# A graph layer stack on one core: the short group of edges moved to the front, adjacency steps moved, row norms of the convolutions on GpSimd, waits of pools by tile

## The chip, the cores and the metric

The kernel runs on one core of one Trainium2 chip. The metric is the device time of one execution in microseconds, as the median of several runs. The engines are called by their short names in the profile: PE (TensorE; PEld are its weight loads), DVE (VectorE), ACT (ScalarE), POOL (GpSimd) and SP (SyncE, here only a DMA queue).

## The reference

There are 1250 nodes of 512 features and 41250 edges (20000 drawn ones in both directions and a loop on each node), sorted by receiver. Two layers follow each other; all is float32.

```python
edge_index = jnp.stack([src, dst])
xn = _layernorm(x, axis=-1)
x = x + gnn0(xn, edge_attr_4, edge_attr_8, edge_index, ...) + mix0(xn, ...)   # messages over edges; linear attention
x = x + ffn0(_layernorm(x), ...)                                              # 8 experts, the best 2 of each node
xn = _layernorm(x, axis=-1)
x = x + gnn1(xn, edge_index, W1, b1, W2, b2) + mix1(xn, ...)                  # two graph convolutions; linear attention
x = x + ffn1(_layernorm(x), ...)                                              # 6 experts, one weighting for all nodes

# gnn0: a product of sender features with edge attributes and a small network's weights, summed by receiver
msg0 = jax.ops.segment_sum(m0, receiver, num_segments=num_nodes)
# gnn1, each of its two convolutions:
norm = dinv[src] * dinv[dst]            # dinv = 1/sqrt(degree), degree from dst
out = jax.ops.segment_sum((x @ W)[src] * norm[:, None], dst, num_segments=n) + b   # then relu
```

## The kernel before

Nodes lie in 10 tiles of 125 rows (`R`, `NT`); `X` holds all of them in SBUF. Edges lie in 323 tiles of 128 (`ET`), and tiles in 47 groups of 7 (`GW`, `NG`). 323 is 46 x 7 + 1: the last group has one tile. The program is written with a framework that draws the semaphores itself and orders each engine's instructions: what is written later may be put earlier on its engine where its inputs allow it. `tc.issue_after(mm.ins)` ties the TensorE instructions of a block behind a matmul, and no other engine's.

The stages, in order of time:

1. **Norm and senders** (to about 53 us). `piece(a, b)` norms the node tiles in four pieces (`PIECES`) and `sender` writes the gather table `xup`. Meanwhile `dg` takes in the receivers, one group to a partition (spare places filled with N by a memset), and the least and greatest receiver of each group give `base`, the group's window of 32 receivers. `rel` is each edge's receiver less that base.
2. **Edges** (about 65 to 591 us), `edges`. Two tiles at a time: `product` gathers sender rows on POOL's queue (`sg`, L443) and multiplies the network's output with `w4b` into `pw` (L448); `messages` makes `msg` on DVE (L454, L457); `gather` multiplies `msg` with the group's factors `sy` into the bank `pd` (L591 to L597). `factors(g)` makes `sy` for a group: two DVE operations and two small ACT multiplies for each tile (L436), in three buffers. At a group's last tile `pd` is copied to `sm` (L601) and added to the table `agg` in HBM by an indirect DMA (L602). Scatters into one table wait for each other, since windows overlap.
3. **Node outputs and router** (591 to about 716 us). `outputs(t)` starts `pz` from a map (L664), reads `agg` back on SP's queue (`ag`, L93/L94 through the helper `spread`), transposes it (L677) and adds. A conditional further pass over the edges stands ahead of it (L640); these data don't take it. `route` and the code after it choose the experts.
4. **Experts** (716 to 1449 us). `unit(u)` takes 256 rows through one expert: 16 steps of first-layer matmuls and a gelu each (L971, L972), then 16 steps of second-layer matmuls (L979). Units 0 to 4 have `counts(g)` among their steps: for each tile of a group a one-hot of receivers times a one-hot of senders (L201), copied to `sa` (L203) and added to the table `adj` in HBM (L204), so `adj` becomes the matrix of edge counts. In unit 5 (`u == NA`) `adjacency(d)` reads node tile d of it back (`ad`, on POOL's queue, two buffers), adds the loop (L932), sums the degrees (L933), casts one half each on DVE and ACT to bf16 (`adb`, one buffer, L936/L937) and transposes it (L943) into `At`. Result rows go to `xrow` by an indirect add (L991). `weights` loads the experts on SP's queue.
5. **Convolutions** (1461 to about 1750 us). Degrees give `dc` (1/sqrt in its second column) and the row `dr`. Node tile by node tile X is read back, normed and scaled into `xs`, and `parts` splits `xs` into three bf16 parts on ACT, POOL (`r`, L1127) and DVE. The plain norm `xn` is transposed into `xT` for the attention. The first aggregation (L1175) takes the node tiles as they come: 12 matmuls for each against the first 500 columns of `At`. The maps L1086 and L1093 and the second aggregation (L1191) follow.
6. **Attention and last experts** (1750 us to the end).

Pools are stacked: a pool that is opened takes the memory of pools closed before it, and its tiles wait for everything in those pools.

Of the kernel before, what the change touches and what calls it, by code (L numbers as in the profile page):

```python
# [20 lines left out]
N = 1250  # L21
# [10 lines left out]
HID = 64  # L32
GW = 7
NG = -(-ET // GW)
W = 32
NPAD = N + W
LO = 313
# [19 lines left out]
def tile_graph_layers(ctx: ExitStack, tc: tile.TileContext, i: dict, out: bass.AP):  # L57
# [1 line left out]
    V, S, T, G = nc.vector, nc.scalar, nc.tensor, nc.gpsimd  # L59

    def pool(stack, name, bufs=1, space=None):
        return stack.enter_context(tc.tile_pool(name=name, bufs=bufs, **({"space": space} if space else {})))

    dram = pool(ctx, "dram", space=DRAM)
    cst = pool(ctx, "cst")
# [18 lines left out]
    def tr_tile(name):  # L84
        return ps_tile("tr", name)
# [5 lines left out]
    def spread(engine, dst, src, at=112):  # L91

        engine.dma_start(dst[:at], src[:at])  # L93
        engine.dma_start(dst[at:], src[at:])  # L94
# [85 lines left out]
    def by_tile(table):  # L180

        return table.rearrange("(c n) f -> n c f", c=4)[:N, :, :].rearrange("(p t) c f -> p t c f", t=NT)

    def counts(sp, g, code, idx, bank):

        n, t0 = min(GW, ET - g * GW), g * GW
        sh = sp.tile([P, GW, P], F16, tag="sh", name="sh")
        q = [P, n, P]
        V.tensor_tensor(sh[:, :n], io[:, None, :].to_broadcast(q), code[:, t0:t0 + n, None].to_broadcast(q),
                        op=OP.is_equal)  # L190
        pa = ps_tile(bank, "pa")
        for j in range(n):
            lo = sp.tile([P, LO + 1], F16, tag="los", bufs=4, name="los")
            if j < 2:

                ab = sp.tile([P, LO + 1], F16, tag="ab", name="ab")
                S.activation(ab, iol, AF.Abs, bias=slo[:, 1, t0 + j:t0 + j + 1], scale=1.0)
                S.activation(lo, ab, AF.Relu, bias=1.0, scale=-1.0)
            else:
                V.tensor_scalar(lo, iol, slo[:, 0, t0 + j:t0 + j + 1], None, op0=OP.is_equal)  # L200
            T.matmul(pa[:, :LO], sh[:, j, :], lo[:, :LO], start=j == 0, stop=j == n - 1)  # L201
        sa = sp.tile([P, LO], F32, tag="sa", bufs=3, name="sa")
        S.copy(sa, pa[:, :LO])  # L203
        G.indirect_dma_start(  # L204
            out=adj[:, :], out_offset=bass.IndirectOffsetOnAxis(ap=idx[:, g:g + 1], axis=0),
            in_=sa, in_offset=None, compute_op=OP.add)

    with ExitStack() as s0:
# [8 lines left out]
        G.dma_start(wu[:, 0, :], i["L0_gnn_W_up0"])  # L217
        G.dma_start(wu[:, 1, :], i["L0_gnn_W_up1"])
        dg = ec.tile([NG, GW * P], I32, name="dg")
        G.memset(dg, N)  # L220
        full = ET // GW
        dr_ = i["dst_row"]
        spread(G, dg[:full, :], dr_[:full * GW * P].rearrange("(g e) -> g e", e=GW * P), full // 16 * 16)
        if full < NG:
            G.dma_start(dg[full:, :(ET - full * GW) * P], dr_[None, full * GW * P:])
        dstc = ec.tile([P, ET], I32, name="dstc")
        G.dma_start(dstc, i["dst_cols"])
        srcc = ec.tile([P, ET], I32, name="srcc")
# [101 lines left out]
        with tc.issue_after(last[0].ins):  # L330
# [33 lines left out]
            EP = NG * GW  # L364
            rel = ec.tile([P, EP], F32, name="rel")
            V.memset(rel, 0.0)
            V.tensor_copy(rel[:, :ET], dstc)
# [13 lines left out]
            def window(code, idx):  # L381

                V.tensor_scalar(bs, base[:, 0, :], float(N), rows, op0=OP.min, op1=OP.add)
                V.tensor_copy(idx, bs)
                V.tensor_scalar(cd[:, 0, :], rel[:, :ET], 0.0, None, op0=OP.is_ge)
                V.scalar_tensor_tensor(cd[:, 0, :], rel[:, :ET], float(W), cd[:, 0, :], op0=OP.is_lt, op1=OP.mult)
                V.scalar_tensor_tensor(cd[:, 1, :], shi, float(W), rel[:, :ET], op0=OP.mult, op1=OP.add)
# [35 lines left out]

        def factors(g):

            n, t0 = min(GW, ET - g * GW), g * GW
            oh = ew.tile([P, GW, W], F32, tag="oh", bufs=3, name="oh")
            V.tensor_tensor(oh[:, :n, :], io[:, None, :W].to_broadcast([P, n, W]),  # L428
                            rel[:, t0:t0 + n, None].to_broadcast([P, n, W]), op=OP.is_equal)
# [148 lines left out]
        def edges(first, idx):  # L578
# [3 lines left out]
            def gather(t, msg):  # L582


                g, j = t // GW, t % GW
                if j == 0:
                    now["d"] = mm_tile("pd")
                sy, d = mask[g], now["d"]
                q = dict(start=j == 0, stop=j == GW - 1 or t == ET - 1)
                mf = msg.rearrange("p b a u -> p (b a) u")  # L590
                T.matmul(d[:W, :SW], sy[:, j, 0, :], mf.rearrange("p a u -> p (a u)")[:, :SW], **q)  # L591
                for c in range(1, 4):
                    T.matmul(d[c * W:(c + 1) * W, :2 * P], sy[:, j, c, :], mf[:, 4:5 + c:c, :],  # L593
                             start=j == 0, stop=False, skip_group_check=True)
                for c in range(1, 4):
                    a = SW + (c - 1) * 64
                    T.matmul(d[c * W:(c + 1) * W, 2 * P:SW], sy[:, j, 0, :], mf.rearrange("p a u -> p (a u)")[:, a:a + 64],  # L597
                             start=False, stop=q["stop"], skip_group_check=True)
                if q["stop"]:
                    sm = ew.tile([P, SW], F32, tag="sm", bufs=5, name="sm")  # L600
                    S.copy(sm, d[:, :SW])  # L601
                    G.indirect_dma_start(  # L602
                        out=agg[:, :], out_offset=bass.IndirectOffsetOnAxis(ap=idx[:, g:g + 1], axis=0),
                        in_=sm, in_offset=None, compute_op=OP.add)
# [7 lines left out]
            for t in range(0, ET, 2):  # L612
# [6 lines left out]
                    ef[b + 2] = attrs(b + 2)  # L619
                if first and at == 10 and b and b - 1 < len(steps):  # L620
                    steps[b - 1]()
                g = t // GW + 1
                if g < NG and g not in mask:
                    mask[g] = factors(g)
                got = [product(x, h[b]) for x in two]
                for x in ready:
                    gather(*x)
# [94 lines left out]
    with ExitStack() as s3:  # L722
# [223 lines left out]
        def unit(u, hu, xu):  # L946
# [6 lines left out]
                    work.setdefault((2 * n + 1) * 16 // len(gs_), []).append(lambda g=g: counts(fk, g, code0, idx0, "acc"))  # L953
            if u == NA:
                for d in range(NT):
                    work.setdefault(8 + (7 * d) // 3, []).append(lambda d=d: adjacency(d))
            n = [0]

            def step(mm):
# [98 lines left out]
    with ExitStack() as s1:  # L1058
# [38 lines left out]
        with ExitStack() as s3:  # L1097
# [24 lines left out]
            def parts(dst, t, src):  # L1122

                d = [x[:R, t, :] for x in dst]
                r = gw.tile([P, D], F32, tag="r", name="r")
                S.copy(d[0], src)
                G.tensor_tensor(r[:R], src, d[0], op=OP.subtract)  # L1127
                S.copy(d[1], r[:R])
                V.tensor_tensor(d[2], r[:R], d[1], op=OP.subtract)
# [7 lines left out]
            g2 = [load_g(i["L1_gnn_W2"][a * 512:(a + 1) * 512, :]) for a in range(2)]  # L1137
            nc.sync.dma_start(gb1, i["L1_gnn_b1"])
            row_bcast(gb2, i["L1_gnn_b2"])
            for t in range(NT):  # L1140
                st = gw.tile([P, V.BN_STATS_DIM], F32, tag="bst", bufs=3, name="n3s")
                V.bn_stats(st[:R], X[:R, t, :])
                V.bn_aggr(mv1[:R, t, :], st[:R])
                S.activation(rs1[:R, t:t + 1], mv1[:R, t, 1:2], AF.Sqrt, bias=eps[:R], scale=1.0)
                V.reciprocal(rs1[:R, t:t + 1], rs1[:R, t:t + 1])
                sc = gw.tile([P, 2], F32, tag="sc", bufs=3, name="sc")
                V.tensor_tensor(sc[:R, 0:1], rs1[:R, t:t + 1], dc[:R, t, 1:2], op=OP.mult)
                V.scalar_tensor_tensor(sc[:R, 1:2], mv1[:R, t, 0:1], -1.0, rs1[:R, t:t + 1], op0=OP.mult, op1=OP.mult)
                xs = gw.tile([P, D], F32, tag="xs", name="xs")
                V.tensor_scalar(xs[:R], X[:R, t, :], mv1[:R, t, 0:1], sc[:R, 0:1], op0=OP.subtract, op1=OP.mult)  # L1150
                parts(xs_, t, xs[:R])
                xn = gw.tile([P, D], F32, tag="xn", bufs=1, name="xn1")
                S.activation(xn[:R], X[:R, t, :], AF.Identity, bias=sc[:R, 1:2], scale=rs1[:R, t:t + 1])
                ps = tr_tile("ptr")
                v = ps[:, :4 * R].rearrange("p (k r) -> p k r", k=4)
                for k in range(4):
                    T.transpose(v[:, k, :], xn[:R, k * P:(k + 1) * P], ident[:R, :R])
                S.copy(xT[:, :, t * R:(t + 1) * R], v)

            def mapped(t, pp):  # L1160
                p_ = gw.tile([P, D], F32, tag="xs", name="prf")
# [435 lines left out]
```

## Time and profile before

| | |
|---|---|
| median of 3 runs | 2175.81 us (2175.56 to 2176.47) |
| the profiled execution's own time | 2173.73 us |
| its span, first to last instruction | 2171.9 us |
| mean granted TensorE clock | 0.973 |
| busy: PE, DVE, ACT, POOL | 2039.8, 891.1, 640.7, 635.3 us |
| 590.6 to 607.7 us: PE busy | 6.57 of 17.1 us |
| unit 5, 1149.3 to 1226.4 us: PE busy | 67.41 of 77.1 us |
| unit 6, 1226.4 to 1282.0 us: PE busy | 55.60 of 55.6 us |
| 1449.5 to 1469.2 us: PE busy | 4.90 of 19.7 us |

The profile is of one execution, and its times count from its first instruction. A row of its timeline gives the start, the duration, the engine, the line, the operation with output and inputs, how often it was done in a row, and in brackets how long the engine had been idle before it and what ended that. "L93" and "L94" are the two halves of `spread`, whoever calls it. In the slices a digit is a share in tenths, and PEclk is the clock that TensorE was granted.

### The profile page before, as it was taken

The numbers are of one execution on the slowest core, as the hardware profiler recorded it, in microseconds if no ns is written. First come the engines' busy times: TensorE is split into PE (matmuls) and PEld (weight loads), VectorE is DVE, ScalarE is ACT, GpSimd is POOL, SyncE is SP. The second block draws the span as 40 slices with busy tenths as digits, with TensorE's granted clock in tenths as the row PEclk, the third lists the DMA queues.
The fourth block names the chain that finished last, engine by engine and source line by source line (L and its number), as shares of the span: only waits on it lengthen the run. The fifth ranks groups of instructions, "written<-read, shape, count | busy, mean of one in ns | idle before, by whom it ended". The sixth has DMA issues, their size and how long they took to land. (4 is left out here: it accounts for less than half of the span.)

```text
span 2171.9 us, 29920 instructions
## 1 busy us (share of the span) xinstructions
PE 2039.8 (94%) x11341; PEld 1109.4 (51%) x11341; DVE 891.1 (41%) x1864; ACT 640.7 (29%) x1665; POOL 635.3 (29%) x589
## 2 busy tenths in 40 slices
PE   7899999989886899999998999978999999999999
PEld 5334444434364646565566666644446655444354
DVE  7688888868757323232233300004000124670000
ACT  3443444434222424243343311115112121241000
POOL 1677777787600323222322211102000020002000
PEclk9899999989997899999999999989999999999999
DMA  8977777757653875958376312413001040200000
GB/s 257 309 203 179 203 200 189 191 137 189 156 146 104 268 225 153 280 145 239 70 235 165 71 25 64 141 31 111 1 0 64 15 95 0 65 7 1 14 14 19
DMA packets 132866, 270.60 MB, mean 125 GB/s; under 512 B 22028, under 2 KB 45396, under 8 KB 132569
## 3 DMA queue, kind: packets, MB, share of 16 engines
q0 software_dynamic: 48048, 124.53, 24.3%
q1 hardware_dynamic: 82952, 140.78, 20.3%
q10 hardware_dynamic: 1694, 3.07, 0.5%
q8 instruction: 99, 1.62, 0.3%
q14 instruction: 73, 0.60, 0.1%
HBM read 248.73 MB, written 44.76 MB: 135 GB/s over the span
## 5 line engine op out<-in xcount | busy, mean ns | idle before, releaser
L443 POOL DMA_INDIRECT sg<-xup,srcc x323 | 311.7, 965 | 165.9 <-issue 63.0
L457 DVE TENSOR_TENSOR msg<-pw,sg 128x768 f32<-128x768 f32 x323 | 305.4, 946 | 0.0
L971 PE MATMUL phd<-hu,ew 128*128 128x256 f32 x1280 | 292.9, 385 | 10.3 <-ACT hd L972 8.0
L979 PE MATMUL pye<-ew,hd 128*128 128x512 f32 x640 | 287.3, 593 | 0.0
L971 PEld LDWEIGHTS phd<-hu,ew 128*128 128x128 f32 x1280 | 243.8, 193 | 50.1 <-ACT hd L972 14.6
L591 PE MATMUL pd<-msg,sy 128*32 128x320 f32 x646 | 215.9, 448 | 29.3 <-DVE msg L457 28.5
L593 PE MATMUL pd<-msg,sy 128*32 128x256 f32 x1938 | 197.8, 394 | 0.0
L448 PE MATMUL pw<-w4b,h 64*128 64x512 f32 x646 | 187.0, 655 | 0.0
L979 PEld LDWEIGHTS pye<-ew,hd 128*128 128x128 f32 x640 | 117.5, 190 | 124.3 <-issue 122.8
L454 DVE TENSOR_TENSOR msg<-pw,sg 128x256 f32<-128x256 f32 x323 | 134.5, 416 | 78.0 <-PE pw L448 38.8
L436 ACT ACTIVATE sy<-oh,y 128x32 f32<-128x32 f32 x646 | 145.9, 312 | 6.1 <-DVE oh L428 3.3
L204 POOL DMA_INDIRECT adj<-sa,idx x47 | 81.6, 1736 | 220.4 <-ACT sa L203 122.9
L200 DVE TENSOR_SCALAR los<-iol,slo 128x314 f16<-128x314 f16 x230 | 58.2, 304 | 199.4 <-PE pa L201 199.4
L591 PEld LDWEIGHTS pd<-msg,sy 128*32 128x32 f32 x646 | 54.4, 109 | 161.5 <-DVE msg L457 93.6
L972 ACT ACTIVATE hd<-phd,b 128x256 f32<-128x256 f32 x160 | 75.8, 474 | 174.5 <-PE phd L971 174.5
L1414 PE MATMUL pyf<-w,hd 128*125 128x512 f32 (+1 forms) x280 | 125.1, 599 | 0.0
L991 POOL DMA_INDIRECT xrow<-yo,slot x23 | 36.3, 1577 | 298.6 <-ACT yo L990 284.9
L1400 PE MATMUL ph<-uT,w 128*128 128x500 f32 (+3 forms) x336 | 120.8, 515 | 1.1 <-ACT hd L1402 1.0
L989 DVE TENSOR_TENSOR yo<-pye,b 128x512 f32<-128x512 f32 x20 | 13.8, 690 | 244.4 <-PE pye L979 231.3
L597 PEld LDWEIGHTS pd<-msg,sy 128*32 128x32 f32 x1938 | 80.7, 112 | 56.0 <-issue 4.0
L412 ACT ACTIVATE h<-ph 128x512 f32<-128x512 f32 (+1 forms) x124 | 68.2, 591 | 135.5 <-PE ph L408 93.7
L597 PE MATMUL pd<-msg,sy 128*32 128x64 f32 x1938 | 94.1, 221 | 0.0
(424 smaller groups left out, 2650.1 us busy)
## 6 DMA issues: line engine op xcount, KB each, us to landing
ew<-in_L_ffn_W SPq DMA_DIRECT2D x104, 1024.0 KB
agg<-zero SPq DMA_DIRECT2D x12, 512.0 KB
adj<-zero SPq DMA_DIRECT2D x12, 512.0 KB
ag<-agg SPq DMA_DIRECT2D x10, 560.0 KB
ad<-adj POOLq DMA_DIRECT2D x10, 547.8 KB
sg<-xup,srcc POOLq DMA_INDIRECT x323
g<-in_L_gnn_W SPq DMA_DIRECT2D x4, 1024.0 KB
w<-in_L_ffn_W SPq DMA_DIRECT2D x4, 852.5 KB
```

The source lines that it names most:

```text
L436: S.mul(sy[:, j, c, :], oh[:, j, :], y4[:, t0 + j, c:c + 1])
L443: G.indirect_dma_start(out=sg, out_offset=None, in_=xup[:, :], in_offset=bass.IndirectOffsetOnAxis(ap=srcc[:, t:t + 1], axis=0))
L448: T.matmul(pw, h[hb:hb + HID, q, (j // 2) * P:(j // 2 + 1) * P], w4b[hb:hb + HID, :], start=True, stop=True)
L454: V.tensor_tensor(msg[:, :, 0, :], w_[:, 0], sg[:, None, :P].to_broadcast([P, 2, P]), op=OP.mult)
L457: V.tensor_tensor(msg[:, :, 1:, :], w_[:, 1, :, None, :].to_broadcast(q), s1[:, None].to_broadcast(q), op=OP.mult)
L591: T.matmul(d[:W, :SW], sy[:, j, 0, :], mf.rearrange("p a u -> p (a u)")[:, :SW], **q)
L593: T.matmul(d[c * W:(c + 1) * W, :2 * P], sy[:, j, c, :], mf[:, 4:5 + c:c, :], start=j == 0, stop=False, skip_group_check=True)
L597: T.matmul(d[c * W:(c + 1) * W, 2 * P:SW], sy[:, j, 0, :], mf.rearrange("p a u -> p (a u)")[:, a:a + 64], start=False, stop=q["stop"], ski ...
L971: mm = T.matmul(ph[:, :UT], ew1[q][:, k, f * P:(f + 1) * P], hu[:, k, :], start=k == 0, stop=k == 3)
L979: mm = T.matmul(py, hd[q][:, f, a * P:(a + 1) * P], ew2[q][:, f, :], start=q == 0 and f == 0, stop=q == 3 and f == 3)
L1400: mm = T.matmul(ph[:m, :c], w1[k][:, f * P:f * P + m], uT[:, k, c0:c1], start=k == 0, stop=k == 3)
L1414: T.matmul(py[:R], hd[f][:m, r0:r0 + R], w2[f // 4][:m, f % 4, :], start=f == 0, stop=f == FT - 1)
```

## The change

- **Groups.** `SH = NG * GW - ET = 6` places are now left free at the front: group 0 holds tile 0 alone, and every other group seven tiles. `of_group` gives a group's number of tiles and its first tile; `counts`, `factors` and `gather` use it, and `rel` is shifted by `SH`. `dg` needs no memset; the spare places of its first row are filled with copies of tile 0's receivers by a further DMA. A pair of tiles can now touch two groups, so a step of the edge loop makes the factors of up to two.
- **Adjacency.** `adjacency(d)` is written at step 12 + 2d of unit 5 instead of 8 + 7d//3: steps 12, 14, ... 30 instead of 8, 10, 12, 15, 17, 19, 22, 24, 26, 29.
- **Convolution rows.** Statistics, square root, reciprocal and scale are done by the pieces of `PIECES` (1, 2, 3 and 4 node tiles) rather than for each tile, and `xn` is made by a `tensor_scalar` on POOL instead of an activation on ACT; the product of mean and scale that the activation's bias needed is gone.
- **Pools.** All pools but the one in HBM get `reuse_waits="tile"`: a tile in reused memory waits only for the earlier tiles whose memory it takes.

```diff
+SH = NG * GW - ET
...
     def pool(stack, name, bufs=1, space=None):
-        return stack.enter_context(tc.tile_pool(name=name, bufs=bufs, **({"space": space} if space else {})))
+        waits = {} if space == DRAM else {"reuse_waits": "tile"}
+        return stack.enter_context(tc.tile_pool(name=name, bufs=bufs, **({"space": space} if space else {}), **waits))
...
+    def of_group(g):
+        t0 = max(g * GW - SH, 0)
+        return (g + 1) * GW - SH - t0, t0
...
     def counts(sp, g, code, idx, bank):
-        n, t0 = min(GW, ET - g * GW), g * GW
+        n, t0 = of_group(g)
...
-        G.memset(dg, N)
-        full = ET // GW
         dr_ = i["dst_row"]
-        spread(G, dg[:full, :], dr_[:full * GW * P].rearrange("(g e) -> g e", e=GW * P), full // 16 * 16)
-        if full < NG:
-            G.dma_start(dg[full:, :(ET - full * GW) * P], dr_[None, full * GW * P:])
+        q = (GW - SH) * P
+        spread(G, dg[1:, :], dr_[q:].rearrange("(g e) -> g e", e=GW * P), (NG - 1) // 16 * 16)
+        G.dma_start(dg[:1, :q], dr_[None, :q])
+        if SH:
+            G.dma_start(dg[:1, q:].rearrange("g (n e) -> g n e", e=P),
+                        bass.AP(tensor=dr_.tensor, offset=dr_.offset, ap=[[0, 1], [0, SH], [1, P]]))
...
             def gather(t, msg):
-                g, j = t // GW, t % GW
+                g = (t + SH) // GW
+                n, t0 = of_group(g)
+                j = t - t0
...
-                q = dict(start=j == 0, stop=j == GW - 1 or t == ET - 1)
+                q = dict(start=j == 0, stop=j == n - 1)
...
-                g = t // GW + 1
-                if g < NG and g not in mask:
-                    mask[g] = factors(g)
+                for g in range((t + SH) // GW + 1, (t + 1 + SH) // GW + 2):
+                    if g < NG and g not in mask:
+                        mask[g] = factors(g)
...
                 for d in range(NT):
-                    work.setdefault(8 + (7 * d) // 3, []).append(lambda d=d: adjacency(d))
+                    work.setdefault(12 + 2 * d, []).append(lambda d=d: adjacency(d))
...
-            for t in range(NT):
-                st = gw.tile([P, V.BN_STATS_DIM], F32, tag="bst", bufs=3, name="n3s")
-                V.bn_stats(st[:R], X[:R, t, :])
-                V.bn_aggr(mv1[:R, t, :], st[:R])
-                S.activation(rs1[:R, t:t + 1], mv1[:R, t, 1:2], AF.Sqrt, bias=eps[:R], scale=1.0)
-                V.reciprocal(rs1[:R, t:t + 1], rs1[:R, t:t + 1])
-                sc = gw.tile([P, 2], F32, tag="sc", bufs=3, name="sc")
-                V.tensor_tensor(sc[:R, 0:1], rs1[:R, t:t + 1], dc[:R, t, 1:2], op=OP.mult)
-                V.scalar_tensor_tensor(sc[:R, 1:2], mv1[:R, t, 0:1], -1.0, rs1[:R, t:t + 1], op0=OP.mult, op1=OP.mult)
...
-                S.activation(xn[:R], X[:R, t, :], AF.Identity, bias=sc[:R, 1:2], scale=rs1[:R, t:t + 1])
+            sc = gc.tile([P, NT], F32, name="sc")
+            for a, b in PIECES:
+                for t in range(a, b):
+                    st = gw.tile([P, V.BN_STATS_DIM], F32, tag="bst", bufs=3, name="n3s")
+                    V.bn_stats(st[:R], X[:R, t, :])
+                    V.bn_aggr(mv1[:R, t, :], st[:R])
+                S.activation(rs1[:R, a:b], mv1[:R, a:b, 1], AF.Sqrt, bias=eps[:R], scale=1.0)
+                V.reciprocal(rs1[:R, a:b], rs1[:R, a:b])
+                V.tensor_tensor(sc[:R, a:b], rs1[:R, a:b], dc[:R, a:b, 1], op=OP.mult)
+                for t in range(a, b):
...
+                    G.tensor_scalar(xn[:R], X[:R, t, :], mv1[:R, t, 0:1], rs1[:R, t:t + 1], op0=OP.subtract, op1=OP.mult)
```

More of the change, by code (lines that the diff above doesn't have):

```diff
@@ L366, in tile_graph_layers @@
             V.memset(rel, 0.0)
-            V.tensor_copy(rel[:, :ET], dstc)
+            V.tensor_copy(rel[:, SH:], dstc)
             rel3 = rel.rearrange("p (g j) -> p g j", j=GW)
@@ L384, in window @@
                 V.tensor_copy(idx, bs)
-                V.tensor_scalar(cd[:, 0, :], rel[:, :ET], 0.0, None, op0=OP.is_ge)
-                V.scalar_tensor_tensor(cd[:, 0, :], rel[:, :ET], float(W), cd[:, 0, :], op0=OP.is_lt, op1=OP.mult)
-                V.scalar_tensor_tensor(cd[:, 1, :], shi, float(W), rel[:, :ET], op0=OP.mult, op1=OP.add)
+                V.tensor_scalar(cd[:, 0, :], rel[:, SH:], 0.0, None, op0=OP.is_ge)
+                V.scalar_tensor_tensor(cd[:, 0, :], rel[:, SH:], float(W), cd[:, 0, :], op0=OP.is_lt, op1=OP.mult)
+                V.scalar_tensor_tensor(cd[:, 1, :], shi, float(W), rel[:, SH:], op0=OP.mult, op1=OP.add)
                 V.scalar_tensor_tensor(cd[:, 1, :], cd[:, 1, :], 1.0, cd[:, 0, :], op0=OP.add, op1=OP.mult)
@@ L424, in factors @@
         def factors(g):
-            n, t0 = min(GW, ET - g * GW), g * GW
+            n, t0 = of_group(g)
             oh = ew.tile([P, GW, W], F32, tag="oh", bufs=3, name="oh")
             V.tensor_tensor(oh[:, :n, :], io[:, None, :W].to_broadcast([P, n, W]),
-                            rel[:, t0:t0 + n, None].to_broadcast([P, n, W]), op=OP.is_equal)
+                            rel[:, SH + t0:SH + t0 + n, None].to_broadcast([P, n, W]), op=OP.is_equal)
             sy = ew.tile([P, GW, 4, W], F32, tag="sy", bufs=3, name="sy")
@@ L582, in gather @@
             def gather(t, msg):
-                g, j = t // GW, t % GW
+                g = (t + SH) // GW
+                n, t0 = of_group(g)
+                j = t - t0
                 if j == 0:
@@ L1139, in tile_graph_layers @@
             row_bcast(gb2, i["L1_gnn_b2"])
-            for t in range(NT):
-                st = gw.tile([P, V.BN_STATS_DIM], F32, tag="bst", bufs=3, name="n3s")
-                V.bn_stats(st[:R], X[:R, t, :])
-                V.bn_aggr(mv1[:R, t, :], st[:R])
-                S.activation(rs1[:R, t:t + 1], mv1[:R, t, 1:2], AF.Sqrt, bias=eps[:R], scale=1.0)
-                V.reciprocal(rs1[:R, t:t + 1], rs1[:R, t:t + 1])
-                sc = gw.tile([P, 2], F32, tag="sc", bufs=3, name="sc")
-                V.tensor_tensor(sc[:R, 0:1], rs1[:R, t:t + 1], dc[:R, t, 1:2], op=OP.mult)
-                V.scalar_tensor_tensor(sc[:R, 1:2], mv1[:R, t, 0:1], -1.0, rs1[:R, t:t + 1], op0=OP.mult, op1=OP.mult)
[L1149 to L1152, printed above, removed]
-                S.activation(xn[:R], X[:R, t, :], AF.Identity, bias=sc[:R, 1:2], scale=rs1[:R, t:t + 1])
[L1154 to L1158, printed above, removed]
@@ new lines, in tile_graph_layers @@
+            sc = gc.tile([P, NT], F32, name="sc")
[8 more added lines that the diff above has]
+                for t in range(a, b):
+                    xs = gw.tile([P, D], F32, tag="xs", name="xs")
+                    V.tensor_scalar(xs[:R], X[:R, t, :], mv1[:R, t, 0:1], sc[:R, t:t + 1], op0=OP.subtract, op1=OP.mult)
+                    parts(xs_, t, xs[:R])
+                    xn = gw.tile([P, D], F32, tag="xn", bufs=1, name="xn1")
+                    G.tensor_scalar(xn[:R], X[:R, t, :], mv1[:R, t, 0:1], rs1[:R, t:t + 1], op0=OP.subtract, op1=OP.mult)
+                    ps = tr_tile("ptr")
+                    v = ps[:, :4 * R].rearrange("p (k r) -> p k r", k=4)
+                    for k in range(4):
+                        T.transpose(v[:, k, :], xn[:R, k * P:(k + 1) * P], ident[:R, :R])
+                    S.copy(xT[:, :, t * R:(t + 1) * R], v)
```

## The prediction

> **What bounds the kernel now.** I read the page first: engine shares, the row of 40 slices, the chain.
>
> ```profile
> span 2171.9 us, 29920 instructions
> PE 2039.8 (94%) x11341; PEld 1109.4 (51%) x11341; DVE 891.1 (41%) x1864; ACT 640.7 (29%) x1665; POOL 635.3 (29%) x589
> PEclk9899999989997899999999999989999999999999
> ```
>
> TensorE is busy 94%: only what takes TensorE's work away, fills its 132 us of idle time or keeps its clock up can show. The change takes no TensorE work away (as many tiles, transposes and matmuls), so it is worth what it does to holes. The waits of PE and the table of 25 us stretches show where they are; three lie in stages that the change touches, and I read each in the timeline.
>
> First the end of the edge stage (a row of the timeline: start, duration, engine, line, operation; in brackets the engine's idle time before it and what ended it):
>
> ```profile
> 590.10 1.58 POOL L602 DMA_INDIRECT agg<-sm,idx  x1 [3.72 <-ACT sm L601]
> 594.52 6.57 PE L664 MATMUL pz<-M,xT 128*125 128x512 f32 x8 [3.95 <-ACTq L640]
> 595.17 1.55 POOL L602 DMA_INDIRECT agg<-sm,idx  x1 [3.48 <-ACTq L640]
> 601.66 0.33 SPq L93 DMA_DIRECT2D ag<-agg  x1
> 607.73 0.86 PE L677 MATMUL pm<-ident,ag 125*128 125x125 f32 x3 [6.65 <-POOL rest L667]
> ```
>
> The two last scatters into agg follow each other within one tile; the second goes out 5.07 us after the first, agg is read back when it has landed (6.5 us), and TensorE waits 6.65 us for it.
>
> Then expert unit 5, where the adjacency is read back:
>
> ```profile
> 1154.13 1.54 POOL L204 DMA_INDIRECT adj<-sa,idx  x1 [6.10 <-ACT hd L972]
> 1159.04 0.83 POOL L93 DMA_DIRECT2D ad<-adj  x1 [0.18 <-issue]
> 1166.04 1.30 ACT L937 CAST adb<-ad 125x625 bf16<-125x625 f32 x1 [9.17 <-DMA ad<-adj]
> 1167.76 8.40 PE L971 MATMUL phd<-hu,ew 128*128 128x256 f32 x24 [7.95 <-ACT hd L972]
> ```
>
> ACT works in order: it stands at the first cast of the adjacency, four gelus into the unit, until the adjacency's rows have landed; the gelus behind it stand too, both PSUM banks fill, and TensorE stops for 7.95 us.
>
> Then the start of the convolutions (the last row is from the table of stretches: length, then PE, PEld, DVE, ACT and POOL busy, clock, DMA):
>
> ```profile
> 1460.92 0.34 SPq L93 DMA_DIRECT2D X<-xrow  x1
> 1461.81 0.16 DVE L1102 TENSOR_REDUCE big<-dg__84 125x1 f32<-125x10 f32 x1 [11.45 <-issue]
> 1464.82 0.69 DVE L1142 BATCH_NORM_STATS2 n3s<-X 125x6 f32<-125x512 f32 x1
> 1493.12 1.36 DVE L1150 TENSOR_SCALAR xs<-X,mv,sc 125x512 f32<-125x512 f32 x1 [1.36 <-POOL r L1127]
> 1469.20:1505.30 36.10, 30.39 (x151) 14.44 (x152) 21.59 (x62) 24.11 (x47) 12.05 (x10) 1.00 0.41 143
> ```
>
> DVE is free from 1450.4 but begins the degrees (L1102) only at 1461.8, when the last scatter's semaphores are in; so the first row's statistics start at 1464.8. From the first aggregation matmul (1469.2) to the end of the first chunk (1505.3) TensorE works 30.39 of 36.1 us, waiting on ACT's rows.
>
> **Part 1, the short group first.** Groups stay 47, scatters 47, and no tile is added. At the end, tile 322 now closes a full group; the group before it closes seven tiles earlier (about 11 us at the 1.6 to 1.8 us that a tile takes), so its scatter has landed. The last scatter then goes out when its copy is done: L601 ends at 591.12, plus 0.28 as at 590.10, so 591.4 instead of 595.17: 3.8 us. It lands before agg is read, and all of that lies on the path: L677 at about 603.9, after the eight L664 matmuls (end 601.1), so TensorE's wait shrinks from 6.65 to 2.8. What is late next is the same transfer.
>
> The clock: after the idle stretch L664's eight matmuls take 6.57 us, where pairs later take 1.02 (4.1 for eight), and the pair after the second wait took 1.59, 0.57 too much. The Trainium skill (TensorE: Matmul & The Clock Gate, The HAM clock gate) says that the array halves its clock after an idle window of some 3.4 us and regains it after as much work. A 2.8 us wait would be under that, so the 0.57 goes; by the rows alone I could claim nothing. I take 0.5. But the rule's price for a drop, 3.4 us at half speed, is 1.7 us; in unit 5 the row above has 24 matmuls in 8.40 us, at 0.217 each 5.2, so 3.2 us. There the row decides.
>
> At the start: a memset of dg (0.89 us) goes and one small DMA (0.54) comes on POOL's queue, which is idle from 8 to 58 us. Three sets of factors are made before the edges, as three buffers allow; they need 30 ACT multiplies instead of 42 (0.22 us apart): 2.6 us less on ACT, but TensorE is busy there until 53.3 and the silu chain follows. Value 0, bounds -2 and +2. In the loop the pairs meet group ends in the same mixture: 0.
>
> In the adjacency counts the last group, at step 30 of unit 4, now has seven tiles: 6 x 0.27 us more TensorE, taken from unit 0. Sum 0, but the last scatter's order relative to unit 5 moves (next part).
>
> **Part 2, adjacency at 12+2d.** Each step issues two POOL DMAs (0.72 + 0.56), on DVE an add, a reduction, a cast and two evictions (0.38 + 1.46 + 1.26 + 0.57), on ACT a cast and two evictions (1.31 + 0.94) and ten transposes (0.9 on TensorE). It is moved by 4, 4, 4, 3, 3, 3, 2, 2, 2, 1 steps of 1.73 us. Only the transposes are tied to a matmul. The rest runs where the scheduler that orders each engine's instructions took its inputs to be ready: the first cast stands behind gelu 4 though it was written at step 8, and the trace has other work far ahead of its place (L659 of the node stage at 442 us). So I expect the cast not to move with its step. What does move: the counts before it end some 1.6 us later against unit 5, about one gelu (1.73), while the real chain of scatters (8.7 and 7.6 us apart, bound by landings) starts 1.6 us earlier against TensorE. Hole 7.95 to about 4.6 us at best, 6.2 if the cast stays: gain 1.7 to 3.4, and 11.2 (7.95 + 3.2) if the cast goes behind the ninth gelu. POOL passes the ad loads over unit 5's scatter (L991) as before, one row more behind it.
>
> The cost: rows come every 3.45 + 0.9 = 4.35 us instead of 4.9. Two ad buffers mean load, add, reduce, cast before the next but one: 0.3 + 5.5 (1200.80 to 1206.34) + 3.1 = 8.9 us for two rows, where 8.7 are there. The head start of four steps covers it, but ad landed in 7.0 us under weights (1159.04 to 1166.06). I take 0.7 us of waits. Net 2.0; bounds -12 (rival 3) and +11.
>
> **Part 3, the convolution's rows.** Per row, ACT loses xn (0.81) and six of ten square roots (0.29): 10 x 2.90 = 29.0 us of ACT become 19.2. POOL gains ten xn. The trace has no such operation: nearest is L667's copy of 256 columns, 0.403, so 0.8 for 512; the upper bound is a two-input row, 1.27. I take 0.9, since it has one tensor. POOL then needs 1.16 + 0.9, under TensorE's 3.04 per row (30.39/10). What queues behind a waiting xn on POOL is the next row's r, which a cast on ACT and m = 1's matmuls wait for.
>
> A rule speaks against this. The row: beside a POOL operation the DVE's xs (L1150) took 1.36 instead of 0.54, and r up to 1.52 instead of 1.16; L1129, with two SBUF inputs, stayed at 0.677 to 0.693. The skill (GPSIMD Engine Reference, Key points) says the two share their SBUF interfaces and contend, for two-port modes and two-input operations alike. By the rule all of POOL (20.6) and of xs and L1129 (12.3) would exclude each other: 33 us, hardly under 36, and the stage gains only at its start. By the rows DVE has 21.6 + 10 x 0.8 at worst = 29.6 us, still under TensorE. I go by the rows, for half of the 5.7 us idle: 2.0 us, bounds -3 and +5.
>
> **Part 4, waits by tile.** It shows at L1102: the degree work and its table load move to about 1451; X's transfer (1460.92) stays, since POOL's bookkeeping after its last scatter holds it. The first statistics come when X lands, some 2.3 us after issue, 1463.3: 1.5 us earlier. Elsewhere waits at stage changes are on data or branches (L640, L1200): 0, bounds -3 (work put ahead into DVE's chain of the router) and +2.
>
> Sum: 3.8 + 0.5 + 2.0 + 2.0 + 1.5 = 9.8 us. Against the profiled execution, 2173.73 us (span 2171.9 and 1.8 around it), 2163.9; the median of the runs, 2175.81, lies 2.1 higher: **2166.0**.
>
> **The rivals.** (1) The main case, chance 0.50, 2161 to 2171. (2) The cast does move: the stop of unit 5 goes whole, 11.2 - 0.7 instead of 2.0: 2157.5. For it: the largest hole that the change touches; against: the cast already runs four steps ahead of its place. 0.20. (3) Slower: the adjacency's feed. If ad lands in 8.5 us instead of 5.5, two rows need 11.9 us, 5.95 each against 4.35; ACT stands at each cast with the gelus behind it, 9 x 1.6 = 14.4 us. That gives 2166 + 2.7 + 14.4 = 2183. It makes the whole slower by over 0.2% from 1.35 us a row, a landing of 8.0 us. For it: 7.0 was seen; against: most land in 5.5 to 5.8. 0.15. (4) The changes in waits don't reach TensorE: rows stretched by POOL, the cast unmoved, waits by tile without effect; only the scatter's 3.8 remains: 2172, within 2170 to 2177. 0.15.
>
> Within 0.2% (4.4 us) a measurement of this kernel can't tell from no change. Faster: 0.49 + 0.20 + 0.04 = 0.73; same 0.12; slower 0.15. The range 2154 to 2178 leaves out the lowest of (2) and nearly all of (3).
>
> **What would show it.** L602's last issue near 591.4 and L677's wait under 3 us (part 1); gelus before the first L937 and L971's longest wait: 4 and 6 to 8 us, 5 and about 4.6, or 9 and none (part 2); ad's landing times and idle time before L937 of the later rows (rival 3); first L1142 near 1463 against X's load at 1460.9, and the first chunk in under 34 us (parts 3 and 4). L1102 still directly after POOL's bookkeeping would make part 4 wrong; an edge loop (69 to 591) longer by over 3 us would make the whole wrong.

## The result and the profile after

| | before | after |
|---|---|---|
| median | 2176.14 us (2174.49 to 2177.79, 6 runs) | 2191.01 us (2184.53 to 2195.48, 6 runs) |
| ratio to before | | 1.0067, 95% interval 1.0055 to 1.0078 |
| the profiled execution's own time | 2173.73 us | 2195.48 us |
| mean granted TensorE clock | 0.973 | 0.967 |

The changed kernel is slower by 15 us at the median, above the range of the prediction. Its profile is of the longest of the six runs, 4.5 us above their median. Line numbers have moved by 2 to 12. From the page:

```profile
span 2193.7 us, 29739 instructions
PE 2052.1 (94%) x11341; PEld 1114.1 (51%) x11341; DVE 889.8 (41%) x1842; ACT 633.5 (29%) x1649; POOL 660.3 (30%) x599
PEclk9899999999996999999999999978999999999999
```

TensorE issues the same 11341 matmuls and is busy 12.3 us longer with them. That points to the clock: in the slices from 1426 to 1536 us it is 0.7 and 0.8, where before had 0.8 and 0.9. POOL is busy 25.0 us longer, for ten operations more and one memset less: some 2.5 us each, where the prediction had 0.9.

Cut at the same instructions in both traces, the span of the profiled executions grew like this:

| stretch | before | after | difference |
|---|---|---|---|
| start to the last product into `pd` (L591, now L602) | 590.1 | 596.1 | +6.1 |
| from there to the first expert matmul (L971, now L982) | 126.4 | 121.0 | -5.4 |
| to the last result row of unit 5 (L989, now L1000) | 509.3 | 509.6 | +0.4 |
| to the first aggregation matmul (L1175, now L1187) | 243.5 | 243.1 | -0.4 |
| to the first chunk's first `ggT` (L1178, now L1190) | 35.5 | 55.2 | **+19.7** |
| to the end | 667.2 | 668.6 | +1.4 |

One stage carries the loss, the first chunk of the convolutions; the longer edge loop and the shorter stage behind it nearly cancel. The places that the prediction showed now look like this. The end of the edges, in the timeline:

```profile
589.43 1.62 POOL L613 DMA_INDIRECT agg<-sm,idx  x1 [0.30 <-issue]
597.41 1.58 POOL L613 DMA_INDIRECT agg<-sm,idx  x1 [6.36 <-ACT sm L612]
600.36 7.82 PE L675 MATMUL pz<-M,xT 128*125 128x512 f32 x14 [3.76 <-ACTq L651]
603.72 0.33 SPq L95 DMA_DIRECT2D ag<-agg  x1
609.45 1.09 PE L688 MATMUL pm<-ident,ag 125*128 125x125 f32 x6 [1.27 <-DVE ag L680]
```

The last scatter leaves 1.3 us after the last L602, where before it left 5.1 us after the last L591; the one ahead of it left 8.0 us earlier. TensorE fills the wait with 14 matmuls instead of 8 and then waits 1.27 us, not 6.65. Unit 5:

```profile
1154.12 1.54 POOL L211 DMA_INDIRECT adj<-sa,idx  x1 [6.17 <-ACT hd L983]
1158.63 1.07 POOL L95 DMA_DIRECT2D ad<-adj  x1
1166.74 1.30 ACT L948 CAST adb<-ad 125x625 bf16<-125x625 f32 x1 [9.31 <-DMA ad<-adj]
1168.46 2.08 PE L982 MATMUL phd<-hu,ew 128*128 128x256 f32 x4 [8.09 <-ACT hd L983]
```

The stop has not moved: ACT stands at the first cast as before, four gelus into the unit, and TensorE stops for 8.09 us (7.95 before). The start of the convolutions:

```profile
1452.42 0.16 DVE L1113 TENSOR_REDUCE big<-dg__84 125x1 f32<-125x10 f32 x1 [1.01 <-DVEq L1063]
1459.16 0.17 DVE L1122 MEMSET on<- 128x128 f32 x1 [6.57 <-DMA xrow<-yo,slot]
1461.88 0.35 SPq L95 DMA_DIRECT2D X<-xrow  x1
1465.00 0.69 DVE L1155 BATCH_NORM_STATS2 n3s<-X 125x6 f32<-125x512 f32 x1 [1.94 <-DMA X<-xrow]
```

The degrees (L1113) no longer wait for the last scatter of results. X's transfer leaves 9.4 us after that scatter, as before (9.5), and the first statistics start when it has landed. Then the first chunk, in the table of stretches, from the first aggregation matmul to the first `ggT` (the first finished sum, scaled and taken out of PSUM), before and after:

```profile
1469.20:1504.70 35.50, 29.79 (x148) 14.14 (x149) 21.02 (x61) 24.11 (x47) 12.05 (x10) 1.00 0.42 146
1469.90:1525.10 55.20, 40.40 (x153) 18.72 (x154) 20.22 (x40) 16.74 (x32) 32.54 (x19) 0.75 0.27 94
```

So of the 19.7 us, 9.1 are idle time of TensorE (14.8 instead of 5.7) and 10.6 are longer work: some 1.0 is the first row's transposes, which before lay just ahead of the stretch, and the rest is the same matmuls at a clock of 0.75 instead of 1.00. Who ends TensorE's waits stands in its list of waits (total, times, longest, in us); before, its transposes waited 3.1 us in all for ACT's `xn`:

```profile
PE ptr L1169 <- POOL xn L1165: 14.4, 7, 4.0
```

The operation itself, from the view of its line (shortest, median and longest in ns, first and last start):

```profile
L1165 POOL TENSOR_SCALAR xn<-X,mv,rs x10: 2072/2198/3284, 1466.6 to 1506.3; 125x512 f32<-125x512 f32 x10
```

And a piece of the timeline of that chunk, which shows what a long operation in POOL's queue sets off:

```profile
1473.59 2.76 POOL L1165 TENSOR_SCALAR xn<-X,mv,rs 125x512 f32<-125x512 f32 x1
1474.16 0.61 ACT L1137 CAST xs<-xs 125x512 bf16<-125x512 f32 x1
1476.40 0.65 PE L1169 MATMUL ptr<-ident,xn 125*128 125x125 f32 x4 [2.44 <-POOL xn L1165]
1477.22 2.07 POOL L1165 TENSOR_SCALAR xn<-X,mv,rs 125x512 f32<-125x512 f32 x1 [0.87 <-DVE n3s L1155]
1479.26 1.16 POOL L1138 TENSOR_TENSOR r<-xs,xs 125x512 f32<-125x512 f32 x1
1480.45 0.62 ACT L1139 CAST xs<-r 125x512 bf16<-125x512 f32 x1 [2.78 <-POOL r L1138]
1481.10 0.69 DVE L1140 TENSOR_TENSOR xs<-r,xs 125x512 bf16<-125x512 f32 x1 [4.68 <-ACT xs L1139]
1481.44 0.30 ACT L1157 ACTIVATE rs<-mv,eps 125x3 f32<-125x3 f32 x1
1481.77 0.17 DVE L1158 RECIPROCAL rs<-rs 125x3 f32<-125x3 f32 x1
```

The cast that `r` needs is done at 1474.8. But two `xn` stand ahead of `r` on POOL, and the second can't begin before TensorE has transposed the first out of the single buffer (1476.40 to 1477.05; the profile names DVE, which had ended at 1476.4). So `r` starts at 1479.26, 4.5 us late; ACT's cast of it waits 2.78 us, DVE's last part 4.68 us. Behind that cast, in ACT's order, stands the square root of the next piece (L1157), whose statistics were ready at 1475.8, and behind DVE's part its reciprocal, without which POOL can't norm the next piece's rows.

The aggregation itself has no use for `xn`. Its matmuls wait because the transposes of `xn` stand among them in TensorE's order: after the last of these (1508.70) TensorE works without a pause to the end of the chunk, with 69 aggregation matmuls from 1509.6 on. What writing the transposes behind the chunk would do wasn't tried.

### The profile page after: what moved, and what is told of

It is laid out like the page before. It is cut to its first block, busy times and chain, and to the rows that moved or that the text cites. A ratio compares the mean times of both kernels' runs of the same rounds, so it can differ in the third digit from the quotient of the medians.

```text
span 2193.7 us, 29739 instructions
## 1 busy us (share of the span) xinstructions
PE 2052.1 (94%) x11341; PEld 1114.1 (51%) x11341; DVE 889.8 (41%) x1842; ACT 633.5 (29%) x1649; POOL 660.3 (30%) x599
## 5 line engine op out<-in xcount | busy, mean ns | idle before, releaser
L982 PE MATMUL phd<-hu,ew 128*128 128x256 f32 x1280 | 291.6, 384 | 9.6 <-ACT hd L983 8.1
L982 PEld LDWEIGHTS phd<-hu,ew 128*128 128x128 f32 x1280 | 243.7, 193 | 49.6 <-ACT hd L983 15.0
L602 PE MATMUL pd<-msg,sy 128*32 128x320 f32 x646 | 215.4, 447 | 35.3 <-DVE msg L466 34.8
L445 ACT ACTIVATE sy<-oh,y 128x32 f32<-128x32 f32 x646 | 145.9, 311 | 10.3 <-DVE oh L437 5.3
L602 PEld LDWEIGHTS pd<-msg,sy 128*32 128x32 f32 x646 | 54.6, 109 | 168.5 <-DVE msg L466 98.5
L1000 DVE TENSOR_TENSOR yo<-pye,b 128x512 f32<-128x512 f32 x20 | 13.8, 690 | 237.4 <-PE pye L990 224.3
```

Of the source, the lines that this page charges most:

```text
L982: mm = T.matmul(ph[:, :UT], ew1[q][:, k, f * P:(f + 1) * P], hu[:, k, :], start=k == 0, stop=k == 3)
```

## The experiments

Theory: `xn` on POOL, at 2.1 to 3.3 us a row, makes the loss. Rivals: that the norming of the rows by pieces makes it; that the edge loop has become longer; that the loss is spread over the parts. The runs came in four sets, each with its own runs of before beside it, which took 2176.06, 2300.06, 2176.25 and 2177.78 us. In the second set (r on DVE, and the three parts alone) the edge loop of all four profiled kernels took over 640 us, for a reason that the record doesn't show. So ratios are compared, and stretches of the profiles; the first chunk with its rows as before took 35.5 us there too.

**xn back on ACT, everything else as changed.**

```
-  G.tensor_scalar(xn[:R], X[:R, t, :], mv1[:R, t, 0:1], rs1[:R, t:t + 1], op0=OP.subtract, op1=OP.mult)
+  S.activation(xn[:R], X[:R, t, :], AF.Identity, bias=sc[:R, t, 1:2], scale=rs1[:R, t:t + 1])   # sc: -mean * rs
```

> The kernel after, with the normed rows xn back on ACT (Identity with scale and bias, 0.81 us each in the profile of before); the pieces, the groups, the adjacency steps and the waits stay as changed. Theory POOL (xn took 2.2 us on POOL where 0.9 was assumed, and its in-order queue, 3.4 us a row with r, sets the pace of the first chunk): the first chunk goes from 52 us back to 36 or less, the time to 2174 us (2170 to 2177). Rival pieces (a piece's rows wait for the statistics and the square root of all its rows, whoever norms them): the chunk stays above 45 us and the time at 2186 to 2191. Rival edges (the 7 us by which the edge loop was longer in the profile are lasting): 2180 to 2184.

The bias is back too, one more small DVE operation for each piece. Measured 2171.93 us, ratio 0.9977 (0.9969 to 0.9986). The chunk:

```profile
1466.00:1500.20 34.20, 30.50 (x148) 14.09 (x149) 18.45 (x42) 23.09 (x41) 11.45 (x10) 0.98 0.45 153
```

With one instruction changed per row the chunk falls from 55.2 to 34.2 us, below before's 35.5, and the clock returns. `xn` on POOL is the cause; the pieces alone don't hurt this stretch.

**The convolutions' part alone, on the kernel before** (the last hunk of the diff, nothing else).

> The kernel before with the convolutions' part alone (pieces, xn on POOL). Theory POOL: the whole loss is here, 2176 + 18 = 2194 us (2190 to 2197), with xn at 2.1 us or more on POOL. Rival edges: a third of the loss is elsewhere, 2184 to 2188.

Measured 2196.45 us, ratio 1.0096 (1.0075 to 1.0118); chunk 54.4 us, `xn` 2.31 us at the median. The part alone costs some 21 us, more than the whole change.

**Groups, adjacency and waits without the convolutions' part** (the changed kernel with the old last hunk).

> The kernel after with the convolutions' rows as before (each row by itself, xn on ACT): groups, adjacency and waits alone. Theory POOL: 2173 us (2170 to 2176), a gain of about 3 from the scatter at the edges' end. Rival edges (the edge loop is lastingly 7 us longer): 2180 to 2184.

Measured 2168.21 us, ratio 0.9955 (0.9940 to 0.9970): a gain of 8 us, more than either theory said. The product of the two ratios is 1.0051, against 1.0067 (1.0055 to 1.0078) measured for the whole.

**One scalar and one operation on POOL.**

```
-  G.tensor_scalar(xn[:R], X[:R, t, :], mv1[:R, t, 0:1], rs1[:R, t:t + 1], op0=OP.subtract, op1=OP.mult)
+  G.tensor_scalar(xn[:R], xs[:R], dc[:R, t, 0:1], None, op0=OP.mult)
```

> The kernel after, with xn on POOL made from the scaled row, xn = xs times the root of the degree, one scalar and one operation in place of two of each; the values are the same up to rounding. If POOL's price is by operations: 1.0 to 1.2 us each, the first chunk near 40 us, the time 2177 to 2182. If it is by scalar operand or by the engine's pass over the row whatever is done: 2.0 us again and 2189 to 2192.

Measured 2188.44 us, ratio 1.0055 (1.0039 to 1.0071); one of the seven executions took 4238.79 us, isn't in the ratio and stays unexplained.

```profile
L1165 POOL TENSOR_SCALAR xn<-xs,dc x10: 1562/1686/2251, 1463.9 to 1500.1; 125x512 f32<-125x512 f32 x10
```

Neither case: one scalar and one operation less save 0.51 us of 2.07 at the shortest, and 1.56 remains. The chunk is 49.4 us.

**The tensor form on POOL.**

```
+  G.tensor_tensor(xn[:R], xs[:R], dc[:R, t, 0:1].to_broadcast([R, D]), op=OP.mult)
```

> The kernel after, with xn on POOL as the product of the scaled row and the root of the degree spread over the row, two tensor operands in place of a scalar one; the values are the same up to rounding. If POOL's price is that of the form with scalars (2.07 us with two operations, 1.56 us with one, against 1.15 us for r with two tensors): 1.15 us each, the first chunk 42 to 46 us, the ratio near 1.002. If POOL's price is set otherwise: 1.5 us or more and a ratio near 1.0055, as with one scalar.

```profile
L1165 POOL TENSOR_TENSOR xn<-xs,dc x10: 1032/1181/1276, 1460.0 to 1491.1; 125x512 f32<-125x512 f32 x10
```

Measured 2178.16 us, ratio 1.0010 (1.0003 to 1.0018), chunk 41.9 us: the first case, and a little better. The same product costs 1.18 us as a product of two tensors (one of them a column spread over the row) and 1.69 with a scalar for each partition: here the form sets POOL's price, and the form that reads more tensors is the cheaper one.

**r on DVE, so that POOL has only xn in the chunk.**

```
-  G.tensor_tensor(r[:R], src, d[0], op=OP.subtract)
+  (V if dst is xs_ else G).tensor_tensor(r[:R], src, d[0], op=OP.subtract)
```

> The kernel after, with the rest r of the split of the conv's scaled rows subtracted on DVE, so that POOL has only xn (2.2 us a row) in the first chunk. If POOL's throughput made the loss (xn and r, 3.4 us a row, against the 3.6 us a row of the whole chunk before): the chunk falls to 36 to 40 us and the time to 2174 to 2178. If it is the chain xn, transposes, copy, with one buffer and each product of a row queued behind those transposes on PE: the chunk stays at 44 to 50 us, 2182 to 2188.

Measured 2299.75 us, ratio 0.9994 (0.9980 to 1.0007). Both have the other parts' gains in them; the chunk answers the question: 49.8 us, the second case. POOL is busy only 19.1 us of these, and TensorE still waits for `xn` eight times, 11.1 us in all. So POOL's throughput alone isn't the cause; how much of the rest is the chain through the single buffer, the next run tests.

**The same with two buffers for xn and one for r.**

> The kernel of the run before it (after, with r on DVE), with two buffers for xn and one for r, which costs the same memory. There POOL waited 13.3 us for PE's transposes and PE 11.1 us for POOL's xn: each row's norming starts only when the transposes of the row before have left the single buffer. If that exchange is what is left of the loss, the chunk falls from 49.8 us to 36 to 42 and the ratio to before by another 0.3 to 0.6%. If the one buffer is not what counts (DVE's doubled work, or PE's order), the chunk stays within 3 us of 49.8.

Measured 2177.17 us, ratio 1.0003 (0.9994 to 1.0012). The chunk is 45.3 us, between the two cases: the buffer was worth 4.5 us of it. The ratio did not fall, but the two runs are of different sets. TensorE still waited 8.2 us for `xn`, now behind others of its kind on POOL: in the last piece POOL runs four in a row for 9.41 us.

The chunk in all kernels, from the table of stretches (idle is length less PE busy):

| kernel | xn, median us | chunk | PE idle | PE busy | clock |
|---|---|---|---|---|---|
| xn back on ACT | ACT 0.81 | 34.2 | 3.7 | 30.5 | 0.98 |
| before | ACT 0.81 | 35.5 | 5.7 | 29.8 | 1.00 |
| tensor form | POOL 1.18 | 41.9 | 9.4 | 32.5 | 0.92 |
| r on DVE, two buffers | POOL 2.08 | 45.3 | 8.3 | 37.0 | 0.81 |
| one scalar | POOL 1.69 | 49.4 | 12.4 | 37.0 | 0.80 |
| r on DVE | POOL 2.07 | 49.8 | 11.1 | 38.7 | 0.78 |
| convolutions' part alone | POOL 2.31 | 54.4 | 16.1 | 38.3 | 0.78 |
| after | POOL 2.20 | 55.2 | 14.8 | 40.4 | 0.75 |

Where `xn` comes from POOL at 1.7 us or more, TensorE's work takes 7 to 11 us longer than before, on top of the idle time: in each of these kernels the lower clock costs about as much as the added waits, or more.

**The other three parts, each alone on the kernel before** (the hunks of the groups, of the steps, of the pools).

> The kernel before with the short group first, and nothing else. Theory groups (the 7.9 us that the three parts without the convolutions gained come from the scatter at the edges' end): 2171 us (2169 to 2173), the last output wait under 2 us, units from about 713. Rival waits (they come from the waits by tile): 2175 to 2177.

Ratio 0.9959 (0.9947 to 0.9971), 9 us of 2300: the short group first carries most of the gain. From the last product to the first expert matmul it takes 120.1 us, where the kernel with the steps alone, otherwise as before there, takes 127.8. The wait for `ag` is 1.71 us (6.84). The rest is the clock again. In the stretch behind that wait the table shows, with the steps alone,

```profile
728.40:750.00 21.60, 21.57 (x115) 15.96 (x115) 12.03 (x33) 6.14 (x11) 1.20 (x3) 0.87 0.54 140
```

and with the short group first

```profile
728.50:750.00 21.50, 21.50 (x136) 15.81 (x137) 14.49 (x40) 7.97 (x15) 1.75 (x4) 1.00 0.58 141
```

136 matmuls in the time of 115, at a clock of 1.00 instead of 0.87.

> The kernel before with the adjacency steps at 12 + 2d, and nothing else. Its cast stands in ACT's queue where it stood, so the hole of 8 us in that unit stays: 2176 us (2175 to 2177.5). Rival (the later steps take work out of the unit's middle, as first forecast): 2174 or less.

Ratio 1.0001 (0.9991 to 1.0012): nothing, as the unmoved cast says; TensorE's stop in that unit is 8.6 us.

> The kernel before with the pools' waits by tile, and nothing else. Theory groups: 2174.5 us (2173.5 to 2176), from the convolutions' preparation that no longer stands behind POOL's bookkeeping. Rival waits: 2171 or less, with the rows of the outputs at the edges' end starting earlier too.

Ratio 0.9983 (0.9974 to 0.9992), 4 us of 2300, between the two cases. Against the kernel with the steps alone, 2.6 us of it lie between the last product and the experts (125.2 against 127.8) and 1.7 between the last gelu matmul and the first aggregation (46.3 against 48.0). Single profiles don't give the first to a microsecond: before had 126.4 there. The product of the three ratios is 0.9943, within the 0.9940 to 0.9970 of the three together.

**Groups and waits, and the first adjacency row's second half cast on DVE.**

```
-  S.copy(ab[:R, h:], own[:R, h:])
+  (V.tensor_copy if d < 1 else S.copy)(ab[:R, h:], own[:R, h:])
```

> Groups and waits as changed, the convolutions' rows and the adjacency's steps as before, and the second half of the cast of the first adjacency row on DVE in place of ACT (DVE waits for that row anyway). If the cast in ACT's queue is what makes the hole of 8 us in that unit, it falls below 2 us and the ratio to before goes from 0.9955 (groups, waits and steps together) to 0.991 to 0.993. If the row's late landing holds the unit in another way (its transposes on PE), the hole moves and the ratio stays at 0.995 to 0.996.

Ratio 0.9952 (0.9939 to 0.9966), the second case: not to be told from the 0.9955 of groups, waits and later steps with ACT's cast. In the list of waits the hole at the gelus is gone and another stands in its place, TensorE at the first row's transposes:

```profile
PE pat L954 <- DVE adb L947: 8.0, 2, 5.2
```

**The same with the steps at 12 + 2d.**

> As the run before it (groups and waits as changed, the convolutions' rows as before, the second half of the first adjacency row's cast on DVE), with the adjacency's steps at 12 + 2d as well. The steps alone left ACT's cast, and with it the hole of 8 us, where they were; the cast alone moved the hole to the first row's transposes on PE (5.2 and 2.8 us). If each of the two needs the other, because the transposes move 7 us later with the steps, both holes go and the ratio to before falls from 0.995 to 0.991 to 0.993. If the unit is held by the rows' landing whatever the order, a hole of 5 us or more is seen again and the ratio stays at 0.995.

Measured 2164.26 us, ratio 0.9939 (0.9925 to 0.9952). Its interval overlaps that of the run before it, and the ratio misses the 0.991 to 0.993 of the first case, so the profile has to say more: from the last result row of unit 4 to that of unit 5 it takes 72.8 us, where before took 76.2, after 76.7 and the cast alone 76.1. One hole of 4.1 us is left, of another kind:

```profile
PE pat L954 <- DVE At L137: 4.9, 2, 4.1
```

There TensorE's later transposes wait for DVE to take the earlier ones out of PSUM. So in these profiles the later steps are worth 3.3 us, but only once the cast is out of ACT's way. This kernel (short group first, waits by tile, steps at 12 + 2d, one cast on DVE, rows of the convolutions as before) has the lowest ratio of those run.

## Why the prediction was wrong, point by point

**Part 3 failed, by its term of 0.9 us for xn.** It was taken from a copy of 256 columns, the wrong kind: a copy has no scalars. The upper bound, a two-input row at 1.27, was no bound either. Measured: 2.20. The next sentence of the step falls with it: POOL needs 1.15 + 2.20 = 3.35 us a row, over the 3.04 that TensorE needs. What the prediction named as queued behind a waiting `xn`, the next row's `r`, is what the timeline shows, 4.5 us late; it was named and not priced. And the clock was priced at the edges' end but not here, where some 10 of the 19.7 us come with it. In place of a gain of 2.0 with a worst case of a 3 us loss, the stage lost 19.7. (The 2.0 was also a slip: half of the 5.7 us idle is 2.9.)

The rule weighed there is that DVE and POOL contend for the SBUF interfaces that they share (the Trainium skill, GPSIMD Engine Reference, Key points); the prediction took it at its strongest, as exclusion. Contention shows, and is small: the ten `xn` took 23.4 us, 2.6 more than ten times the shortest (up to 3.28 instead of 2.07, beside DVE's work), and DVE's `xs` took 0.76 us at the mean, 0.69 before. The size of the loss came from the operation's own price and the chain.

**Part 1 was right in mechanism and too small.** The scatter goes out 3.8 us earlier against the last product (1.3 instead of 5.1), as predicted, and the wait is under 3. The clock was mis-sized at 0.5 us: from the first transpose of `ag` to the experts the ten kernels with the short group first took 105.8 to 107.7 us, the four without it 108.5 to 110.1, and in the pair above the clock behind the wait was 1.00 instead of 0.87. By its ratio the part was worth some 9 us, where 4.3 were forecast. That the loop itself costs nothing isn't certain: from first to last product before took 521.1 us and the convolutions' part alone 519.7; the eight kernels with the short group first outside the second set took 522.1 to 528.3, the changed kernel most. In the second set two with it took 643.9 and 646.7 and two without it 642.1 and 649.1. So 1 to 7 us stay unsettled. The sign that the prediction gave for "the whole wrong", a loop longer by over 3 us, was seen in after's profile and was not the cause.

**Part 2 was right that the cast doesn't move, and wrong in its gain of 2.0.** The `ad` load starts 1.0 us earlier against the unit, but the cast starts 8.1 us after it instead of 7.0; TensorE's stop stays. Both rivals with the adjacency failed: the cast didn't move with the steps, and the unit was only 0.5 us longer than before.

**Part 4**: the degrees started at 1452.4, where 1451 was said, and the statistics 0.9 us earlier against the last scatter of results (12.6 us behind it, 13.4 before), not 1.5. The value 0 "elsewhere" was wrong by some 1 to 3 us between edges and experts.

Without part 3 the forecast was 7.8 us of gain, and without the convolutions' part 7.9 were measured. That was luck: the 2.0 of the adjacency didn't come, and the groups gave twice their forecast.

None of the rivals named the right loss: the slower one was put on the adjacency's feed.

**What stays open.** With xn on ACT, the changed kernel stands at 0.9977, though without the convolutions' part it is at 0.9955 and its chunk is 2.5 us shorter. The profiles show a difference of 5.0 us from the first `ggT` to the last layer's statistics, at the conditional after the convolutions. Pieces with xn on ACT:

```profile
1744.45 36.76 PE L1293 MATMUL pkT<-xT,g 128*128 128x500 f32 x96 [3.66 <-DVEq L1213]
```

without the convolutions' part:

```profile
1743.37 33.84 PE L1291 MATMUL pkT<-xT,g 128*128 128x500 f32 x96 [1.62 <-ACTq L1211]
```

A longer stop at the branch, and a lower clock after it. But the stretch is as short with pieces in both kernels that have r on DVE (376.6 us in each, against 376.5), so it isn't the pieces as such. What makes the difference wasn't tried.

## What to carry to other kernels

Price an operation that moves to another engine by a row of that engine in the same form (scalars, operations, length), and where there is none, let the bound reach to a multiple. Then write out the loop that the operation closes: its buffer, the queue it stands in, what stands behind it, and whether its engine still keeps the pace of the one that bounds. And count TensorE's repeated short waits at some twice their length: here the clock fell with them and cost about as much again, or more.

## What the runs showed of the hardware

- POOL, float32, 125 x 512: two tensors 1.15 us; a tensor and one scalar for each partition, one operation, 1.56 us at the shortest; two scalars and two operations 2.07 us, up to 3.28 us beside DVE's work. ACT does the last in 0.81 us.
- Repeated waits of 1.3 to 4.0 us took the clock down and up again. Cut where the clock changes, the first chunk after reads:

| from, to (us) | PE busy | clock |
|---|---|---|
| 1473.9, 1477.3 | 0.96 of 3.4 | 1.00 |
| 1477.3, 1484.2 | 5.46 of 6.9 | 0.51 |
| 1484.2, 1487.6 | 1.74 of 3.4 | 1.00 |
| 1487.6, 1491.0 | 1.40 of 3.4 | 1.00 |
| 1491.0, 1497.8 | 4.79 of 6.8 | 0.50 |
| 1497.8, 1501.2 | 2.42 of 3.4 | 1.00 |
| 1501.2, 1504.6 | 1.28 of 3.4 | 1.00 |
| 1504.6, 1514.9 | 8.55 of 10.3 | 0.50 |
| 1514.9, 1525.0 | 10.10 of 10.1 | 1.00 |

  The clock fell behind 3.4 us with 0.96, 1.40 and 1.28 us of work, and not behind those with 1.74 and 2.42; each time it came back in this table, the 3.4 us ahead had been all work (3.0 of 3.4 when it came back at 1473.9). The rule used in the prediction (the Trainium skill, TensorE: Matmul & The Clock Gate, The HAM clock gate) puts the fall behind an idle window of some 3.4 us. By that a chain of shorter waits, none of them a whole such window ahead of a fall, would have cost no clock; here a stretch that was more than half idle was enough.
- The edge loop took 642 to 649 us in the four kernels of the second set and 520 to 528 in the others. With the steps alone, TensorE was idle at `pd` for 46 us that the profile puts down to no releaser; the stages behind the loop took the same as before within 3 us. The record names the same chip for the second and the third set, so it isn't shown that the chip makes the difference; the cause is open.
